# The fence inside the score products: an instruction of its own, or a wait on the product behind it

## The chip, the cores and the metric

The kernel runs on one core of one Trainium2 chip. The metric is device time in microseconds from start to end of one execution; three runs are given. A profiled execution has its own time and a span, the time from its first to its last recorded instruction.

## What is computed

Two residual layers on an image `x` of 4 x 256 x 64 x 64, in float32. Each normalizes its input by groups of channels and adds an attention over it; the second also has a 7 x 7 depthwise convolution of the values and an output projection.

```
# layer 0: 4096 queries, 1024 keys from a strided convolution
attn = einsum('bhdn,bhdm->bhnm', q, k + pos)
attn = softmax(attn * scale, axis=-1)
out  = einsum('bhdm,bhnm->bhdn', v, attn)
x = x + out
# layer 1: 1024 queries and 1024 keys in each of 4 areas
attn = softmax(einsum('bihd,bjhd->bhij', q, k) * scale, axis=-1)
out  = einsum('bhij,bjhd->bihd', attn, v) + dwconv7(v)
x = x + conv1x1(out, w_proj)
```

There are 8 heads of 32 channels, and the scores of either layer have 4096 x 1024 entries for each head and image. The score products are therefore made eight times for 4 images and 2 layers, each with a contraction of only 32.

## The kernel before

**Tiles.** A *unit* is 512 queries of four heads of one image and layer; the four heads lie on four groups of 32 partitions. There are 8 blocks (4 images, 2 layers) of 16 units. A unit has 8 *steps*, one for 128 keys each. A step needs, for each of its four heads, the scores of 128 keys by 512 queries (a PSUM bank each), their exponentials, and the product of these with the values. `score_product` (L419) makes the scores of one head as two products of 64 keys each (`WIDE`), so that they go to two halves of the array's columns; heads lie on four groups of its rows. A float32 product stands in the trace as two passes, each with a weight load (`LDWEIGHTS`) and a product (`MATMUL`).

**Phases.** PSUM has room for six banks of scores, in three pairs `s0`, `s1`, `s2`. A phase of the main loop therefore makes one and a half steps: a *full* tile of 512 queries by four heads, which fills two pairs (`a` for heads 0 and 2, `b` for heads 1 and 3), and a *half* tile, 256 queries by four heads, which fills the third pair (`c`). In pair `c` heads 0 and 1 share a bank, and so do heads 2 and 3: each has half of the columns. There are 683 phases, 682 of them with a half tile.

**The order of a phase on TensorE** is written out by hand, and the whole main loop is in a mode in which no scheduler moves anything. `scores(f)` (L430) emits

1. the half tile's heads 1 and 3 (four products of 256 columns), each of which adds 1 to a semaphore of the kernel's own, `in_bank`; `bank_count` is what it comes to;
2. the full tile's heads 0 and 2, then 1 and 3 (eight products of 512 columns);
3. a fence: a wait until `in_bank` has the count of all products of part 1 so far;
4. the half tile's heads 0 and 2 (four products of 256 columns).

The fence keeps two heads from writing one bank at the same time[...]. The framework tracks dependencies by itself and adds waits for them; products of part 1 are put in a group (`first_{f}`) that it leaves alone, and `declare_fence` tells it which instruction stands for the order between that group and what follows.

Then come the exponentials on ScalarE (L465 for the full tile, in two; L476 for the half tile), each of 128 x 1024 elements. The next pieces on TensorE are a part of other work (a projection at L167, a convolution by band matrices at L1046, the sums for the divisors at L509) if one is due, and the products with the values of the *previous* phase (`weighted`, L490). VectorE adds the exponentials up (L500), for the divisors. Loads of other inputs are issued from SyncE, small transfers for the divisors from GpSimd.

A full tile's pair can be written once ScalarE has read what stood in it before; that is the wait "ACT p" at L423.

Of the kernel before, what the change touches and what calls it, by code (L numbers as in the profile page):

```python
# [60 lines left out]
def direct_path(  # L61
# [19 lines left out]
    V, S, G, T = nc.vector, nc.scalar, nc.gpsimd, nc.tensor  # L81
# [87 lines left out]
    def ps_banks(n, name):  # L169
        return psum.tile([P, 2, CH], FP, tag=f"s{n}", name=name, bufs=1)  # L170
# [230 lines left out]
    in_bank, bank_count = tc.alloc_semaphore("in_bank"), [0]  # L401

    def acc_of(g):
        if g not in accs:
            accs[g] = pool.tile([P, 4, CH], FP, tag="acc", name="acc", bufs=2)
        return accs[g]

    def pair_of(h):
        return slice(2 * (h % 2), 2 * (h % 2) + 2)

    def acc_half(g, u):
        return acc_of(g).rearrange("p (l b) (u n) -> p u b l n", l=2, u=2)[:, u]

    def parts_of(f):

        full, half = (3 * f + 1) // 2, (3 * f // 2 + 1, 0) if f % 2 == 0 else (3 * f // 2, 1)
        return (full if full < last else None), (half if half[0] < last else None)

    def score_product(out, s, h, cols):  # L419
        g, j = divmod(s, NKT)  # L420
        rows, unit = slice(HD * h, HD * h + HD), units[g]
        return [
            T.matmul(  # L423
                out[n : n + WIDE], lhsT=unit[2]()[rows, unit[0], j * P + n : j * P + n + WIDE],
                rhs=unit[1]()[rows, cols], start=True, stop=True,
            )
            for n in range(0, P, WIDE)
        ]

    def scores(f):  # L430

        full, half = parts_of(f)
        a, b, c = [ps_banks(n, "s") for n in ((0, 1, 2) if f % 2 == 0 else (0, 2, 1))]
        every = slice(0, CH)

        def half_product(h):

            u = half[1]
            return score_product(
                c[:, h // 2, HC * (h % 2) : HC * (h % 2) + HC], half[0], h, slice(HC * u, HC * u + HC)  # L440
            )

        if half is not None:
            for h in (1, 3):
                for first in half_product(h):
                    first.then_inc(in_bank, 1)
                    tc.add_to_no_dep_group(f"first_{f}", first.ins)
                    tc.no_tile_sem_insts.add(first.ins.name)
                    bank_count[0] += 1
        for h in (0, 2, 1, 3):  # L450
            score_product((a, b)[h % 2][:, h // 2, :], full, h, every)
        if half is not None:
            fence = T.wait_ge(in_bank, bank_count[0])
            tc.declare_fence(fence.ins, group=f"first_{f}")
            for h in (0, 2):
                half_product(h)

        def exp_full(n):
            g, j = divmod(full, NKT)
            if j == 0:  # L460
                p = acc_of(g)[:, pair_of(n), :]
            else:
                p = pool.tile([P, 2, CH], FP, tag="p", name="p", bufs=PB)
            made_p[full, n] = p
            S.activation(p, (a, b)[n], AF.Exp, scale=SCALE)  # L465

        def exp_half():
            if half is None:
                return
            (g, j), u = divmod(half[0], NKT), half[1]  # L470
            if j == 0:
                p = acc_half(g, u)
            else:
                p = pool.tile([P, 2, CH], FP, tag="p", name="p", bufs=PB).rearrange("p b (l n) -> p b l n", l=2)
            made_p[half[0], 2 + u] = p
            S.activation(p, c.rearrange("p b (l n) -> p b l n", l=2), AF.Exp, scale=SCALE)  # L476

        return [lambda: exp_full(0), lambda: exp_full(1), exp_half]
# [677 lines left out]
    f = step = 0  # L1156
    before, credit = [], 0.0
    while f < PHASES or before or plan or side or quick or norms_left or to_add or to_divide:
        now[0], phase[0] = step, f
        exps = scores(f) if f < PHASES else [lambda: None] * 3  # L1160
        mine = []
        if f < PHASES:
# [668 lines left out]
```

## Time and profile before

| | |
|---|---|
| three runs, median (lowest to highest) | 3108.29 us (3106.65 to 3117.26) |
| the profiled execution, its own time | 3110.89 us |
| its span | 3108.5 us |
| granted clock of TensorE, mean | 0.996 |
| score products (L423), two groups | busy 552.0 and 549.7 us, mean 499 and 497 ns |
| products with the values (L490), two groups | busy 450.9 and 450.6 us, mean 486 and 487 ns |
| exponentials of the full tile (L465) | 1194 and 172 of 1026 and 1024 ns |
| exponentials of the half tile (L476), first group | 598 of 1037 ns |
| ScalarE idle before the first of these, for TensorE's scores | 416.7 us |

How to read it: one record of a load is on row PEld, one of a product on row PE. Products overlap, as four groups of rows and two of columns work beside each other, so that the busy time of TensorE is the union of its records and their mean durations cannot be summed. The end of a product is modelled from its size, its start is measured. A wait by an instruction of its own is a record of the sequencer, `EVENT_SEMAPHORE`, and counts as no busy time.

### The profile page before, as it was taken

The page shows a single profiled execution, that of the slowest core. Times are in us where ns is not written, and L with a number is a line of the kernel's source. Part 1 is how long each engine was busy: PE and PEld are TensorE (multiplying, and loading weights), DVE is VectorE, ACT ScalarE, POOL GpSimd, SP SyncE. Part 2 cuts the span into 40 slices and gives each one's busy share as a digit, 9 for nine tenths or more (in the row PEclk, how much of TensorE's full clock was granted, in tenths as well). Part 3 has the DMA queues.
Part 4 walks back from the last instruction along what each step waited for, and adds up shares of the span by engine and source line. Part 5 has one row for each costly group of instructions (what it writes and reads, how often), then busy time and mean ns, then how long its engine had stood idle before and what let it go on. Part 6 is the DMA issues. An engine that isn't in the chain of part 4 may idle for free. (4 is left out here: it accounts for less than half of the span.)

```text
span 3108.5 us, 110007 instructions
## 1 busy us (share of the span) xinstructions
PE 3059.6 (98%) x47254; PEld 1269.4 (41%) x47254; DVE 2517.8 (81%) x2721; ACT 2459.3 (79%) x2988; POOL 484.9 (16%) x921
## 2 busy tenths in 40 slices
PE   9999999999999999999999999999999999999998
PEld 6444333444444444333444444443444444343332
DVE  3788977789887787777788888777888888888888
ACT  3888877888888888788888787787777787778875
POOL 0111111111121111111112111111111111111111
PEclk9999999999999999999999999999999999999999
DMA  5244433566335455777865667667655565542222
GB/s 188 56 96 114 106 80 72 110 146 156 93 95 136 140 156 141 185 181 194 206 171 145 160 171 189 169 172 181 169 152 149 146 164 145 154 105 74 55 68 64
DMA packets 648323, 423.71 MB, mean 136 GB/s; under 512 B 411772, under 2 KB 556636, under 8 KB 647832
## 3 DMA queue, kind: packets, MB, share of 16 engines
q1 hardware_dynamic: 619384, 380.11, 48.3%
q0 software_dynamic: 28448, 36.48, 4.9%
q8 instruction: 379, 6.21, 0.9%
q14 instruction: 112, 0.92, 0.1%
HBM read 318.32 MB, written 98.09 MB: 134 GB/s over the span
## 5 line engine op out<-in xcount | busy, mean ns | idle before, releaser
L500 DVE TENSOR_TENSOR acc<-acc,p 128x1024 f32<-128x1024 f32 x1790 | 2115.1, 1220 | 437.2 <-PE av L490 187.4
L465 ACT ACTIVATE p<-s 128x1024 f32<-128x1024 f32 x1194 | 1161.4, 1026 | 428.1 <-PE s L423 416.7
L476 ACT ACTIVATE p<-s 128x1024 f32<-128x1024 f32 x598 | 620.0, 1037 | 0.3 <-DVE acc L500 0.3
L423 PE MATMUL s<-q,k_A 32*64 32x256 f32 (+1 forms) x10928 | 552.0, 499 | 15.8 <-ACT p L465 14.8
L423 PE MATMUL s<-q,k_B 32*64 32x512 f32 (+1 forms) x10912 | 549.7, 497 | 2.4 <-ACT p L465 1.7
L490 PE MATMUL av<-p,v_A 128*32 128x256 f32 (+1 forms) x4784 | 450.9, 486 | 0.0
L490 PE MATMUL av<-p,v_B 128*32 128x512 f32 (+1 forms) x4776 | 450.6, 487 | 0.0
L423 PEld LDWEIGHTS s<-q,k_A 32*64 32x64 f32 x10928 | 258.8, 130 | 358.9 <-issue 135.9
L423 PEld LDWEIGHTS s<-q,k_B 32*64 32x64 f32 x10912 | 260.3, 130 | 345.6 <-issue 140.9
L535 POOL DMA_DIRECT2D rb<-recs x508 | 252.9, 503 | 517.4 <-DMA recs<-few 440.3
L533 POOL DMA_DIRECT2D recs<-few x127 | 70.2, 553 | 1408.9 <-DVE sums L532 1242.0
L490 PEld LDWEIGHTS av<-p,v_B 128*32 128x32 f32 x4776 | 149.5, 110 | 262.8 <-issue 236.9
L490 PEld LDWEIGHTS av<-p,v_A 128*32 128x32 f32 x4784 | 149.7, 110 | 228.2 <-issue 186.4
L465 ACT ACTIVATE acc<-s 128x1024 f32<-128x1024 f32 x172 | 167.2, 1024 | 84.9 <-PE s L423 84.8
L525 POOL DMA_DIRECT2D few<-rows x127 | 71.5, 563 | 468.3 <-DMA rows<-den_sb 462.0
L509 PE MATMUL den<-acc,ones 128*32 128x512 f32 x1024 | 139.8, 604 | 3.2 <-DVE acc L500 2.6
L167 PE MATMUL ops<-cv,wp_sb 128*32 128x512 f32 x1024 | 126.5, 605 | 4.9 <-DVE cv L814 2.9
L167 PE MATMUL q0ps<-hq,wq_sb 128*32 128x512 f32 x1024 | 125.1, 598 | 1.8 <-ACT q L662 1.4
L167 PE MATMUL k1ps<-h,wqkv_sb 128*32 128x512 f32 x1024 | 123.8, 598 | 2.6 <-ACT k_B L731 1.9
L167 PE MATMUL q1ps<-h,wqkv_sb 128*32 128x512 f32 x1024 | 124.3, 598 | 0.0
L167 PE MATMUL vals_ps<-hv,wqkv_sb 128*32 128x512 f32 x1024 | 124.1, 598 | 0.0
L167 PE MATMUL k0ps<-taps,wkv 128*32 128x256 f32 x2048 | 123.7, 382 | 0.0
(103 smaller groups left out, 2154.8 us busy)
## 6 DMA issues: line engine op xcount, KB each, us to landing
rows<-vals SPq DMA_DIRECT2D x384, 195.9 KB
rb<-recs POOLq DMA_DIRECT2D x508, 64.0 KB, 3.4
share<-vals SPq DMA_DIRECT2D x128, 195.9 KB
vala<-vout SPq DMA_DIRECT2D x128, 144.0 KB
vals<-vout SPq DMA_DIRECT2D x128, 144.0 KB
vc<-vala SPq DMA_DIRECT2D x64, 288.0 KB
band<-mats SPq DMA_DIRECT2D x96, 176.0 KB
hq<-in_x SPq DMA_DIRECT2D x32, 512.0 KB
```

Source lines behind the costliest of these rows:

```text
L167: T.matmul(out[cols, :], lhsT=lhsT[:, cols], rhs=rhs, start=start, stop=stop)
L423: T.matmul(out[n : n + WIDE], lhsT=unit[2]()[rows, unit[0], j * P + n : j * P + n + WIDE], rhs=unit[1]()[rows, cols], start=True, stop=True,)
L465: S.activation(p, (a, b)[n], AF.Exp, scale=SCALE)
L476: S.activation(p, c.rearrange("p b (l n) -> p b l n", l=2), AF.Exp, scale=SCALE)
L490: T.matmul(out, lhsT=v[:, j, unit[0] * P + HD * h : unit[0] * P + HD * h + HD], rhs=rhs, start=(j == 0 and not u), stop=(j == NKT - 1), sk ...
L500: V.tensor_add(to, to, p)
L509: T.matmul(dens[g][HD * h : HD * h + HD, :], lhsT=ones, rhs=p(h), start=(n == 0), stop=(n == len(sets) - 1),)
L525: G.dma_start(few[:, 0, :], rows.rearrange("h (q n) -> (h q) n", n=CH // HD))
L533: G.dma_start(recs.rearrange("h (q n) -> (h q) n", n=CH // HD), few[:, 1, :])
L535: G.dma_start(rb[HD * h : HD * h + HD, :], recs[h : h + 1, :].to_broadcast([HD, CH]))
```

## The change

```
         for h in (0, 2, 1, 3):
             score_product((a, b)[h % 2][:, h // 2, :], full, h, every)
         if half is not None:
-            fence = T.wait_ge(in_bank, bank_count[0])
-            tc.declare_fence(fence.ins, group=f"first_{f}")
-            for h in (0, 2):
-                half_product(h)
+            second = [product for h in (0, 2) for product in half_product(h)]
+            second[0].wait_op(in_bank, bank_count[0], "sem-ge")
+            tc.declare_fence(second[0].ins, group=f"first_{f}")
```

The four products are emitted as before and in the same order. The wait for `in_bank`, against the same count, is now an attribute of the first of them (head 0, first 64 keys), and that product is what the framework knows as the fence. No instruction stands between the full tile's products and it.

In the program the framework's own waits change with it. The fence had been an instruction of TensorE's sequencer, with a count of its own (a semaphore named `PE_sequencer`); later instructions that follow on the fence waited for this count as well. There were 674 such waits before the first product of the full tile's heads 1 and 3, and 680 before the exponential of the half tile on ScalarE. They are gone. The order of all instructions is otherwise the same on all engines.

## The prediction

> **What bounds the kernel now.** First the busy shares and the clock on the page, then the waits of TensorE, then the timeline of one phase, then its weight loads alone.
>
> ```profile
> PE 3059.6 (98%) x47254; PEld 1269.4 (41%) x47254; DVE 2517.8 (81%) x2721; ACT 2459.3 (79%) x2988; POOL 484.9 (16%) x921
> ...
> PEclk9999999999999999999999999999999999999999
> ...
> PE s L423 <- ACT p L465: 16.5, 23, 5.5
> PE ops L167 <- DVE cv L814: 2.9, 1, 2.9
> ```
>
> TensorE is busy for 98% of the span at nearly full clock, and the longest of its waits sums to 16.5 us of 3108.5. ScalarE and VectorE have about a fifth of the span to spare. The chain that ended last cannot show this: it reaches back only some 27 us. So what one phase of the loop takes on TensorE is what the kernel takes, 683 times over. A phase:
>
> ```profile
> 1507.71 0.40 PE L490 MATMUL av<-p,v_A 128*32 128x256 f32 x4
> 1508.04 1.58 PE L423 MATMUL s<-q,k_A 32*64 32x256 f32 x32
> 1509.55 0.62 PE L167 MATMUL q0ps<-hq,wq_sb 128*32 128x512 f32 x2
> ...
> 1508.04 0.64 PEld L423 LDWEIGHTS s<-q,k_A 32*64 32x64 f32 x24 [0.41 <-ACT p L476]
> 1508.93 0.24 PEld L423 LDWEIGHTS s<-q,k_A 32*64 32x64 f32 x8 [0.25 <-issue]
> ...
> L453 PEldq EVENT_SEMAPHORE  x682: 51/51/51, 74.0 to 3076.7; - x171
> L423 PEldq EVENT_SEMAPHORE  x675: 51/51/51, 69.0 to 3078.0; - x169
> ```
>
> The reader is to see that the sixteen score products stand as 32 records (two passes each), that their loads come in two bursts, and that the second burst, the eight loads behind the fence, follows 0.25 us of idle loader put down to "issue". Products look dense nonetheless. Taking the start of every record from the trace (ns from the phase's first product, median of the phases without a disturbance) shows where the density ends:
> - heads 1 and 3 of the half tile: pass one at 0 to 20, pass two at 267 to 287;
> - heads 0 and 2 of the full tile: 27 to 47 and 507 to 527; heads 1 and 3 of it: 483 to 502 and 912 to 932;
> - heads 0 and 2 of the half tile, behind the fence: pass one at 936, 943, 949, 956, of 377, 407, 407, 407 ns; pass two at 1155, 1191, 1198, 1204, of 374 ns.
>
> Elsewhere four products of 256 columns last 374 ns and start 7 ns apart. Behind the fence three of them last 33 more, and the second pass shows a step of 36 where 7 is usual. The cause stands in the loads:
>
> ```profile
> 1508.93 0.13 PEld L423 LDWEIGHTS s<-q,k_A 32*64 32x64 f32 x1 [0.25 <-issue]
> ...
> 1508.91:1508.95 0.04, 0.02 (x1) 1.00 0.00 0
> 1508.95:1508.96 0.01, 0.01 (x1) 1.00 0.00 0
> 1508.96:1508.97 0.01, 0.01 (x2) 1.00 0.00 0
> 1508.97:1508.98 0.01, 0.01 (x4) 1.00 0.00 0
> ```
>
> (The number in brackets counts loads under way in the stretch.) The first load starts at 1508.927, the second at 1508.963, 36 later, then 7 apart. A product begins some 52 ns after its load where it has to wait for it (the phase's first product: 425 ns instead of 374, so 51), hence the 33 ns. The four updates of in_bank land at 1508.696, .738, .781, .823; the fence executes at .852, 28 to 29 after the last (so in 643 of the 682), and the next load starts 76 ns after that (in 641). The wait itself is long met by then[...].
>
> [...] 69 loads of the full tile that waited for ScalarE late in a phase start 41 to 42 ns after its update, and the loads behind them follow 7 ns apart. [...] loads at 269 for products at 483. [...] here the four are 42 apart, and I use 42.
>
> **The change, part by part.** (1) 682 fences go; their wait sits on the first load of heads 0 and 2. The nearest row is the load that waits for ScalarE in mid-phase:
>
> ```profile
> 185.02 0.23 PEld L423 LDWEIGHTS s<-q,k_A 32*64 32x64 f32 x16 [0.41 <-issue]
> 185.45 0.21 PEld L423 LDWEIGHTS s<-q,k_A 32*64 32x64 f32 x8 [0.20 <-ACT p L476]
> 185.91 0.23 PEld L423 LDWEIGHTS s<-q,k_A 32*64 32x64 f32 x8 [0.25 <-issue]
> ...
> 185.02 1.58 PE L423 MATMUL s<-q,k_A 32*64 32x256 f32 x32
> ```
>
> There a load was let go 0.43 us into the phase while products ahead of it (pass two of the full tile's heads 0 and 2, at 507) had not begun; the phase still took 1.58. So with a last update at .823 I put the first load at .823 + 42 = .865, or .850 with the 27 that loads at the start of a phase show, and the others 7 apart. To be ready for a product at 936 (1508.976) a load must start by .924, the fourth by .944. All are early by 50 or more, and even a spacing of 36 for the second would do. Pass one then starts at 936 to 956 without loss; pass two 216 later, at 1152 to 1172. The last product starts at 1172 instead of 1204: **32 ns a phase**.
>
> Is that on the path? The next stage's first product comes 304 ns after the last score product in 625 of the 679 phases with all records, be it a projection, a denominator or the weighted sum: 216 of streaming and 88 of turning to another shape of tile. So it moves with it. What is late next is the full tile's heads 1 and 3: last start 932, streaming 430, end at 1362, against 1420 now and 1388 then. The cover of 26 ns holds, and 58 would be the most that could ever be won here.
>
> How many phases: in 633 of the 679 the last product starts 1204 to 1206 after the first; in the other 46, mostly a late load of the full tile (released by ScalarE at some 840 or 915) sets the end, and I take nothing there. 633 x 32 = 20.3 us. Where a phase before such a late one ends earlier, ScalarE is still the one to wait for, so up to 46 x 32 = 1.5 us is given back: 18.8 us.
>
> (2) The 675 waits for the fence's own count before the full tile's second pair cost nothing now: in the phase shown that record lies at 1508.062 between loads at .058 and .065, the usual 7. If they were not covered, losing them would win 51 each, 34 us; I take 0, and see no way to a loss. (3) Some 680 like them go from ScalarE's queue before the half tile's exponential (records there: median 38 ns). They lie in an engine that idles 428 us before its exponentials of the full tile; 0, and a few us at most through the 46 late phases. (4) The order of all other work on all engines stays, DMA queues too.
>
> Sum, against the profiled execution (span 3108.5; its own time 3110.9 includes 2.4 around it): 3108.5 - 18.8 = 3089.7 of span. The median of the runs shown, 3108.29, lies 2.6 under the profiled time, so 3108.3 - 18.8 = 3089.5 is the time forecast.
>
> **Rivals.** *No gain, 3108.* The next stage could be set by something other than the last score product, or the held load costs as much as the fence (76 and more). For it: the turn of 88 ns is the same after every stage, so I know it only as a constant. Against it: 304 follows the last product, and a held load was measured at 42. *Half gain, 3099.* The first load starts in time, but the second trails it; with .865 for the first it is late only from a spacing of 66 on, and no held load shows more than 7.
>
> *Slower, 3123.* [...] a load with an open wait might be let through only behind the second pass of the full tile's heads 1 and 3, which stands ahead of it and starts at 1508.952 to .972, so at .979 instead of .927. With 52 from load to product and 7 between loads, the four first passes begin at 991 to 1012 and the last second pass at 1228 instead of 1204: 633 x 24 = +15 us. It decides from a first load at .955 on. For it: no load of this trace had to wait for TensorE's own products. Against it: the load at 185.45 and twenty like it, let go at 301 to 435 with products ahead of them unstarted, in phases of unchanged length.
>
> *Swallowed by ScalarE, 3108.* If the exponentials paced the phases, the gain would only be waited out. Three of about 1.03 us make 3.1 in a mean phase of 4.42; only the shortest phases (3.74) come near, and there the full tile's load is released at 280 to 300 after the phase's start. It is needed by 431, so 32 less does not reach it.
>
> **How the numbers follow.** Forecast as worked out 0.85, half gain 0.03, no gain 0.05, swallowed 0.02, slower 0.05. The unknown costs make the likeliest case 3083 (all 682 phases, and some of ScalarE's late ones shortened) to 3097; the half gain takes the range to 3101. No change that can be told from this measurement is within 0.3%, 9.3 us: faster 0.87 (the forecast, and most of the half gain), same 0.08 (the rest of it, no gain and swallowed), slower 0.05.
>
> **What would show it.** Right: no fence records, loads of heads 0 and 2 at about 810 to 830 from the phase's start, all four first passes of 374 ns, a phase of 1.55 instead of 1.58, the next stage still 0.30 behind. Wrong: a load after 885, a phase still 1.58, or more than the 46 phases set by ScalarE.

## The result and the profile after

The changed kernel takes 3092.91 us (median of 5 runs, 3090.81 to 3096.16), the kernel before 3112.92 us in the runs taken with it (3106.65 to 3117.26). The ratio is 0.994, 95% interval 0.9924 to 0.9955: 20 us less, between 14 and 24. The profiled execution of the changed kernel took 3092.91 us, with a span of 3090.8.

The page and the longest waits of TensorE of the changed kernel:

```profile
PE 3036.6 (98%) x47254; PEld 1282.2 (41%) x47254; DVE 2516.2 (81%) x2721; ACT 2455.2 (79%) x2988; POOL 483.1 (16%) x921
PE   9999999999999999999999999999999999999998
...
PEclk9999999999999999999999999999999999999999
```

```profile
PE s L423 <- ACT p L464: 18.2, 23, 5.9
PE den L508 <- DVE acc L499: 4.3, 2, 2.2
PE ops L167 <- DVE xm L828: 3.2, 1, 3.2
```

Work and bound are the same: as many products, TensorE at 98%, a granted clock of 0.996 in both, waits for other engines about as small as they were (the longest sums to 18.2 us, 16.5 before). What fell is the busy time of TensorE's products, by 23 us; those of VectorE and ScalarE changed by some 4 us at most. The same phase as the one shown of before, in the timeline:

```profile
1498.16 1.55 PE L423 MATMUL s<-q,k_A 32*64 32x256 f32 x32
1499.64 0.64 PE L167 MATMUL q0ps<-hq,wq_sb 128*32 128x512 f32 x4
...
1498.16 0.64 PEld L423 LDWEIGHTS s<-q,k_A 32*64 32x64 f32 x24 [0.41 <-issue]
1498.99 0.27 PEld L423 LDWEIGHTS s<-q,k_A 32*64 32x64 f32 x8 [0.19 <-PE s L423]
```

The stage is 1.55 us long instead of 1.58, and the next begins 1.48 after its start instead of 1.51. The second burst of loads is put down to "PE s", the products whose updates it waits for, and no longer to "issue". How close they stand, from the number of loads under way in short stretches:

```profile
1498.97:1498.99 0.02, 0.00 (x0) 1.00 0.00 0
1498.99:1499.00 0.01, 0.01 (x2) 1.00 1.10 424
1499.00:1499.01 0.01, 0.01 (x3) 1.00 0.09 14
1499.01:1499.02 0.01, 0.01 (x4) 1.00 0.09 14
```

Four loads have started within 0.02 us of the first; before, the second came 36 ns behind the first. And of the wait instructions at the score products only the very first is left:

```profile
L423 PEldq EVENT_SEMAPHORE  x1: 51/51/51, 65.8 to 65.8; - x1
```

From the starts of all records, in ns from a phase's first product (median of the phases without a disturbance):

| | before | after |
|---|---|---|
| last update of in_bank | 783 | 783 |
| fence executes | 811 | none |
| first and second load behind it | 887, 923 | 825, 832 |
| half tile, heads 0 and 2, pass one | 936 to 956, of 377, 407, 407, 407 ns | 936 to 956, of 374 each |
| their pass two | 1155, 1191, 1198, 1204 | 1152, 1158, 1165, 1172 |
| next stage, behind the last of these | 304 | 304 |
| phases without a disturbance, of the 679 that the prediction counts | 633 | 636 |

The first held load starts 42 or 43 ns after the last update in 642 of the 682 phases. Added up over all 682 phases with a half tile, the time from a phase's first score product to its last fell from 843.6 to 823.0 us, by 20.6. The other parts of the two profiled spans differ by little and in both directions: the lead-in is 3.1 shorter, the steps from score products to the next stage 1.8 longer, the work between 1.8 and the steps back to score products 2.2. Hence the 17.7 us between the spans.

### The profile page after: what moved, and what is told of

It reads as the page before. It is cut to its first block, busy times and chain, and to the rows that moved or that the text cites. A ratio compares the mean times of both kernels' runs of the same rounds, so it can differ in the third digit from the quotient of the medians.

```text
span 3090.8 us, 108514 instructions
## 1 busy us (share of the span) xinstructions
PE 3036.6 (98%) x47254; PEld 1282.2 (41%) x47254; DVE 2516.2 (81%) x2721; ACT 2455.2 (79%) x2988; POOL 483.1 (16%) x921
## 5 line engine op out<-in xcount | busy, mean ns | idle before, releaser
L423 PE MATMUL s<-q,k_A 32*64 32x256 f32 (+1 forms) x10928 | 543.5, 497 | 17.1 <-ACT p L464 16.2
L423 PE MATMUL s<-q,k_B 32*64 32x512 f32 (+1 forms) x10912 | 537.8, 494 | 2.8 <-ACT p L464 2.0
L423 PEld LDWEIGHTS s<-q,k_A 32*64 32x64 f32 x10928 | 266.3, 131 | 342.6 <-ACT p L464 73.3
L423 PEld LDWEIGHTS s<-q,k_B 32*64 32x64 f32 x10912 | 267.2, 130 | 325.6 <-PE s L423 60.8
L167 PE MATMUL v0ps<-wkv,taps 128*32 128x256 f32 x2048 | 124.0, 386 | 0.0
```

The source lines that it names most:

```text
L167: T.matmul(out[cols, :], lhsT=lhsT[:, cols], rhs=rhs, start=start, stop=stop)
L423: T.matmul(out[n : n + WIDE], lhsT=unit[2]()[rows, unit[0], j * P + n : j * P + n + WIDE], rhs=unit[1]()[rows, cols], start=True, stop=True,)
```

## The experiments

Each ratio is to the kernel before, run on the same chip. The theory is that the products waited for loads that came late, the first 76 ns behind the fence and the second 36 behind the first. Rival A says that the instruction as such, or the waits for its own count elsewhere, cost the time; rival B that it was the number of instructions.

### The fence kept, its last update earlier (e1)

```
-            for h in (1, 3):
-                for first in half_product(h):
-                    first.then_inc(in_bank, 1)
...
-                    bank_count[0] += 1
+            early = [product for h in (1, 3) for product in half_product(h)]
...
+            early[-1].then_inc(in_bank, 1)
+            bank_count[0] += 1
```

> The fence stays an instruction, as before, but only the last of the four products ahead of it adds to the semaphore, so that the last update lands some 126 ns earlier (three updates of 42 ns fewer). Theory (what costs is that the loads behind the fence start late): fence at about 686 from the phase's first product instead of 812, loads from 761 on, all before the 884 at which the first is needed; the phase's last product at 1172, and the kernel 20 us faster than before, ratio 0.994, just as with the change. Rival A (the instruction as such, or the waits for its own count on TensorE and ScalarE, costs the time): all of these stay, so ratio 1.000. Rival B [...]: ratio 1.000.

Measured: 3093.44 us, ratio 0.9945 (0.9929 to 0.9961). All 682 fences are there, as one line's records show, and so are the 675 waits for their count:

```profile
L453 PEldq EVENT_SEMAPHORE  x682: 51/51/51, 74.6 to 3058.3; - x171
```

```profile
L423 PEldq EVENT_SEMAPHORE  x675: 51/51/51, 69.7 to 3059.7; - x169
```

A phase in the timeline:

```profile
1403.65 0.64 PEld L423 LDWEIGHTS s<-q,k_A 32*64 32x64 f32 x24 [0.41 <-issue]
1404.46 0.28 PEld L423 LDWEIGHTS s<-q,k_A 32*64 32x64 f32 x8 [0.17 <-issue]
...
1403.65 1.55 PE L423 MATMUL s<-q,k_A 32*64 32x256 f32 x32
```

The loads still follow the fence as late as before (76 ns behind it, the second 35 behind the first), but it comes earlier, and they start at 810 and 845 from the phase's start instead of 887 and 923, and the last product starts at 1172. The single update lands at 705, where I had put it at 657: the four landings are 42 ns apart, but three updates fewer bring the last one forward by only 78, from 783 to 705. So a gain that cannot be told from the change's is to be had with the fence in place: 12 to 22 us by the interval, where rivals A and B expected none. What counts here is when the loads start. That it is not the number of updates is seen from the changed kernel, which has the gain with all four.

### The fence kept, nothing waits for its count (e3, e6)

The first try told the framework that the product is the fence, and left the wait instruction where it was:

```
-            fence = T.wait_ge(in_bank, bank_count[0])
-            tc.declare_fence(fence.ins, group=f"first_{f}")
-            for h in (0, 2):
-                half_product(h)
+            T.wait_ge(in_bank, bank_count[0])
+            second = [product for h in (0, 2) for product in half_product(h)]
+            tc.declare_fence(second[0].ins, group=f"first_{f}")
```

> The fence stays an instruction with four updates, but the framework is told that the product behind it is the fence, so that nothing waits for the fence's own count: 675 wait instructions on TensorE and about 135 on ScalarE go, as with the change. Theory: loads still at 887 and 923, the last product at 1204, ratio 1.000 to before, within 0.002. Rival A (these waits cost the time): ratio 0.994. Rival B [...]: about half of the gain, 0.997.

Measured: 3090.61 us, ratio 0.9932 (0.9918 to 0.9947), against the expectation of the theory. But the experiment did not do what it was meant to: the trace has no record of the fence, the load behind it carries the wait (in all 682 phases), and at the score products' line stands one wait instruction, as in the changed kernel:

```profile
L423 PEldq EVENT_SEMAPHORE  x1: 51/51/51, 66.2 to 66.2; - x1
```

Nobody counts the completion of this wait. What was executed *is* the changed kernel, so the experiment decides nothing on the rivals. It suggests that the fence was an instruction of its own because of the count that the framework hung on it. The second try gave the wait an update of a semaphore that nobody reads:

```
-            T.wait_ge(in_bank, bank_count[0])
+            T.wait_ge(in_bank, bank_count[0]).then_inc(passed, 1)
```

> The fence with four updates, with nothing in the program waiting for its count (so without the 675 and some 680 waits), but with an update of a semaphore that nobody reads, so that it stays an instruction on the chip: 682 records. Theory [...]: fence at 812 from the phase's first product, loads at 887 and 923, last product at 1204, ratio to before 1.000 within 0.002. Rival A (the waits for the fence's count cost the time): 1172 and ratio 0.994.

Measured: 3108.63 us, ratio 0.9986 (0.9980 to 0.9993). Now the fence is there, and a phase looks as before:

```profile
L454 PEldq EVENT_SEMAPHORE  x682: 51/51/51, 73.3 to 3078.8; - x171
```

```profile
1414.27 0.64 PEld L424 LDWEIGHTS s<-q,k_A 32*64 32x64 f32 x24 [0.41 <-ACT vout L971]
1415.16 0.24 PEld L424 LDWEIGHTS s<-q,k_A 32*64 32x64 f32 x8 [0.25 <-issue]
...
1414.28 1.58 PE L424 MATMUL s<-q,k_A 32*64 32x256 f32 x32
```

Fence at 811, loads at 887 and 923, last product at 1205. So here an update of its own was enough to keep the wait an instruction: 682 records, and none for the fence in e3. The waits for the count, about 1350 of them, are gone and bring 0.07 to 0.2%, 2 to 6 us; where that little comes from, the trace doesn't tell (the phases' own time is 842.9 us against 843.6).

### A wait instruction beside the carried wait, long met (e4)

```
+            if bank_count[0] > 4:
+                T.wait_ge(in_bank, bank_count[0] - 4)
             second = [product for h in (0, 2) for product in half_product(h)]
             second[0].wait_op(in_bank, bank_count[0], "sem-ge")
```

> The changed kernel, and in the place of the fence a wait instruction again, but for the count of the phase before, which has been met for microseconds. Theory [...]: the sequencer passes it early in the phase, loads at about 826, last product at 1172, ratio to before 0.994. Rival A (any instruction between the products costs its 51 to 76 ns[...]): last product at 1204, ratio 1.000.

Measured: 3093.81 us, ratio 0.9938 (0.9922 to 0.9955). The instruction is there in 681 phases:

```profile
L454 PEldq EVENT_SEMAPHORE  x681: 51/51/51, 75.9 to 3061.5; - x171
```

In 632 of them it executes within the first 0.5 us of its phase. In the phase looked at that is 97 ns after the first product; the held load starts at 824, as with the change, and the last product at 1171:

```profile
1405.26 0.27 PEld L423 LDWEIGHTS s<-q,k_A 32*64 32x64 f32 x8 [0.19 <-PE s L423]
...
1404.44 1.54 PE L423 MATMUL s<-q,k_A 32*64 32x256 f32 x32
```

A wait instruction in this place, executed that early, has no price that these runs can tell (3093.81 us against 3092.91 with the change). It has no update of its own and stayed an instruction all the same, 681 records, here in front of a load that carries a wait already.

### Two waits (e5, e7)

```
+            T.wait_ge(in_bank, bank_count[0])
             fence = T.wait_ge(in_bank, bank_count[0])
```

> Before, with the wait instruction twice in a row, the second met when it is reached. Theory: the first load starts one such record, 51 ns, later, 938 instead of 887, now after the 884 at which it is needed, and the second 36 behind it at 974; passes begin at 990 to 1040, the last product at 1256 instead of 1204, and 636 phases of 52 make 33 us, ratio 1.011. Rival A (the lateness of the loads is not what the products wait for): 1204 as before, ratio 1.000.

Measured: 3108.31 us, ratio 0.9998 (0.9989 to 1.0007). The added wait has no record of its own: one record a phase, 682 in all, stands for both, and the experiment decides nothing. With an update on the first, both stay:

```
+            T.wait_ge(in_bank, bank_count[0]).then_inc(passed, 1)
             fence = T.wait_ge(in_bank, bank_count[0])
```

> Before, with a second wait instruction ahead of the fence, for the same count, with an update of its own, so that both stay instructions. Theory: the first load starts 51 to 76 ns later, at 938 to 963 instead of 887, past the 884 at which it is needed, the second 36 behind it; the last product at 1256 to 1281 instead of 1204, 52 to 77 ns in each of 636 phases, 33 to 49 us, ratio 1.011 to 1.016. Rival A (the products do not wait for these loads): 1204 and ratio 1.000.

Measured: 3198.27 us, ratio 1.0276 (1.0262 to 1.0290), some 86 us more where 33 to 49 were expected. In the timeline:

```profile
1450.05 0.64 PEld L424 LDWEIGHTS s<-q,k_A 32*64 32x64 f32 x24 [0.41 <-ACT vout L973]
1451.09 0.23 PEld L424 LDWEIGHTS s<-q,k_A 32*64 32x64 f32 x8 [0.41 <-issue]
...
1450.05 1.74 PE L424 MATMUL s<-q,k_A 32*64 32x256 f32 x32
```

The second burst of loads now waits 0.41 us instead of 0.25. The second wait executes at 966, 156 ns after the first at 810, although its condition is met; the load follows 77 behind it, at 1043, and the last product starts at 1360 instead of 1204: 156 ns more, so that the lateness passes through one to one. (Added up over the phases of the two profiled executions, the time from first to last score product grew by 103 us, and all that lies outside shrank by 17; hence the 86.) The theory holds; the price of a second such instruction, 156 and not 51 to 76, was wrong. What these 156 ns are made of stays open.

### Earlier than needed (e2)

The changed kernel with the single update of e1.

> The changed kernel with one update instead of four: the held load is let go at about 705 + 42 = 747 instead of 826. Theory: the products behind it wait for the array (936), not for loads, so 1172 as with the change, and ratio to before 0.994; loads that are earlier still win nothing. Rival B (every ns of an earlier load counts, or fewer updates help by themselves): last product before 1172, ratio under 0.990.

Measured: 3089.84 us, ratio 0.9926 (0.9913 to 0.9940), not told apart from the changed kernel's 0.9924 to 0.9955. All the loads of the phase now stand in one row:

```profile
1402.05 1.09 PEld L423 LDWEIGHTS s<-q,k_A 32*64 32x64 f32 x32 [0.41 <-issue]
...
1402.05 1.55 PE L423 MATMUL s<-q,k_A 32*64 32x256 f32 x32
```

In this phase the held load starts at 748, 78 ns earlier than with the change, and the last product at 1172 all the same. Here, where the loads were in time already, 78 ns more won nothing.

### The held load where it is needed early (e9)

```
-        for h in (0, 2, 1, 3):
-            score_product((a, b)[h % 2][:, h // 2, :], full, h, every)
+        for h in (0, 2):
+            score_product(a[:, h // 2, :], full, h, every)
+        odd = [product for h in (1, 3) for product in score_product(b[:, h // 2, :], full, h, every)]
         if half is not None:
-            second = [product for h in (0, 2) for product in half_product(h)]
-            second[0].wait_op(in_bank, bank_count[0], "sem-ge")
...
+            odd[0].wait_op(in_bank, bank_count[0], "sem-ge")
```

> The changed kernel, with the wait carried by the first product of the full tile's heads 1 and 3 instead of the half tile's head 0. The same held load, but here needed at 431 and let go at 826. Theory (the price of a held load is its lateness where it is needed, and nothing else): these products start at about 878 instead of 483, last second pass at about 1329 with 430 of streaming, so the next stage starts some 371 ns later in 636 phases, 236 us, ratio about 1.076. Rival C (the array finds other work ahead of a held load, as the half tile's heads 0 and 2 stand behind it): under 1.03.

Measured: 3299.83 us (2 runs), ratio 1.0600 (1.0580 to 1.0619).

```profile
1498.21 1.91 PE L423 MATMUL s<-q,k_A 32*64 32x256 f32 x32
1500.05 0.42 PE L491 MATMUL av<-p,v_A 128*32 128x256 f32 x4
...
1498.20 0.23 PEld L423 LDWEIGHTS s<-q,k_A 32*64 32x64 f32 x16 [0.41 <-ACT vout L972]
1499.03 0.26 PEld L423 LDWEIGHTS s<-q,k_A 32*64 32x64 f32 x16 [0.59 <-PE s L423]
```

The loader stands for 0.59 us, the held load starts at 825, and the last product at 1326, as expected to 3 ns. The next stage follows 517 after that (the last pass is now one of 512 columns), 1843 from the start against 1508 before: 335 a phase. The 371 of the expectation were counted from the changed kernel, although the ratio is to the one before. 633 x 335 = 212 us; the spans differ by 190. The missing 22 us lie outside the score products: the steps to the next stage grew by 130 us where 633 x 213 make 135, the work between shrank by 5, the steps back to score products by 10, and lead-in and end by 3. TensorE's waits for ScalarE at L423 sum to 9.4 us instead of 16.5. Some 670 waits for ScalarE, which the first load of these heads carries in the other kernels, stand here as instructions ahead of it. They mostly execute 21 ns after the phase's first product, long before the held load is let go. The same wait, on the same kind of instruction and let go at the same moment, costs nothing that is seen in one place and 190 us in another.

## Why the prediction was right

- **The bound.** TensorE's own pace (98% busy in both profiles), a phase at a time: right. A phase's stage lost 32 ns, and the run lost 20 us where 18.8 were forecast. That the two lie so close is partly luck: the interval of the gain is 14 to 24 us. The time forecast, 3089.5, lies 3.4 below the measured one, since the kernel before took 4.6 us more in the runs taken with the change than in the three from which the forecast was counted.
- **What was late.** That products behind the fence waited for their loads, and these for the fence, was read from a step of 36 ns among steps of 7. e1 shows it from one side (the same fence, with its loads at 810 and 845, costs nothing that is seen: ratio 0.9945), e7 from the other (loads 156 ns later put the last product 156 later), and e6 shows that the waits for the fence's count are no part of it beyond 2 to 6 us. Why the loads follow the fence 76 and 36 ns behind is not shown.
- **The price of a held load.** 42 ns after the last update, taken from loads that waited for ScalarE; measured 42 or 43, the first load at 825 as worked out, spacing 7. That the load would be let go past waiting products, which the slower rival doubted, is shown by its start at 825 with those products starting at 912.
- **What is late next.** The array itself: 936 for the first of these products. e2 shows it, since loads 78 ns earlier don't move it. The cover of 26 ns by the full tile's heads 1 and 3 was not put to the test. Where they do come last, in e9, the next stage follows their last product by 517, which is their 430 of streaming and again a turn of 87 or 88, so that the turn holds behind another last product too.
- **The waits costed at nothing** were put at 0, and at a few us at most on ScalarE. By e6 they are worth 2 to 6 us, little but not nothing. Part of the 20 us may therefore be theirs; e1, in which they all stay, gains 12 to 22.
- **Given back to ScalarE.** 1.5 us was taken off for it, and the starts of the records show that it happens. 37 undisturbed phases stand ahead of a disturbed one in both profiled executions. In 24 of them the last score product came some 33 ns earlier, but the next phase began at most 12 earlier: its first load starts 41 to 43 ns after ScalarE's update in both executions, so ScalarE was waited for instead. In six more the next phase began 32 earlier and then took 30 longer. These 30 make about 0.9 us. The prediction took 3.74 us for the shortest phases; these 24 are of 3.17 to 3.28, near the 3.1 of three exponentials, and in them the gain was indeed swallowed. The other parts of the two spans differ by more than this term (3.1 us in the lead-in alone), so the run's time does not show it.

## What to carry to other kernels

In this kernel a wait as an instruction of its own executed 28 ns after the last update; the next load came 76 ns behind it and the one after that 36 more, and where they were needed sooner this cost 32 ns a phase. Carried by the load, the wait put the load 42 ns after the last update, with the next 7 behind; loads behind a held one waited with it in e9, whose loader stood for 0.59 us. Look for it where a step in the starts of records breaks an otherwise even row, and compare the moment at which the load starts with the moment at which the array is free: only the difference was to be won here (32 ns, and nothing from loads 78 ns earlier still). An earlier signal did as well as a cheaper wait (e1, ratio 0.9945 against 0.994), and both together brought nothing more that can be told (e2, 0.9926).

## What was not expected of the hardware

- Two wait instructions without an update of their own left no record: in e3 the load behind carries the wait in all 682 phases, in e5 one record a phase, 682 in all, stands for two waits. With an update they stayed (682 records in e6, twice 682 in e7). One without stayed too, ahead of a load that carries a wait already (e4, 681 records). What decides it was not tested further.
- A second wait instruction for the same count executed 156 ns behind the first (e7, ratio 1.0276), whereas one for a count long met, executed within the first 0.5 us in 632 phases, cost nothing that is seen (e4, 0.9938 against the change's 0.994).
- Updates of one semaphore by four products that start within 20 ns of each other land 42 ns apart (655, 698, 740, 783), so the fourth update lands 128 ns after the first. With one update, by the last product alone, it lands at 705, only 78 earlier. Where the other 50 of the 128 belong stays open.
